# A graph attention kernel: where picked tiles leave their PSUM banks, and where score maxima are issued

## Chip, cores and metric

One core of a Trainium2 chip. The time is that of one execution on the device in microseconds; times are medians of several runs.

## The reference

Three layers of a graph attention over 6250 nodes and 206250 edges, sorted by their target node, with 64 features, then log_softmax, a residual and a layer norm. For each layer, cut to what matters:

```python
q, k, v = x @ Wq + bq, x @ Wk + bk, x @ Wv + bv
e = edge_attr @ We
alpha = sum(q[dst] * (k[src] + e), -1) / sqrt(64)
p = exp(alpha - segment_max(alpha, dst)[dst])
w = p / segment_sum(p, dst)[dst]
x = relu(segment_sum((v[src] + e) * w[:, None], dst) + x @ Ws + bs)   # layer_norm after layers 0 and 1
```

So each edge needs the row of its source node, which is a gather.

## The kernel before

The edges lie in tiles of 128, six tiles to a chunk, four chunks to a **unit**; 67 units of four chunks and a short one go through each layer. The loop over units (line 1883) works on three at a time: for unit u its rows are transposed (`turn`, line 1676 on TensorE, two featT copies on ScalarE, line 1679), for u-1 the scores are made (`scores`, line 1689 on TensorE; a running maximum on VectorE, line 1696, for each half; then the bound, line 1709, and one Exp on ScalarE, line 1710) and turned (`weights`, line 1724; probT, line 1727), and for u-2 the weighted sums are taken (`sums`, line 1736, with the copy of line 1743). Each unit is done in four **quarters**, one chunk's `turn` in each; quarter 2 begins with the first half of `weights`, and ends with the second.

**Where rows come from.** Most tiles are gathered by GpSimd's indirect DMAs (line 601), which wait for a small copy on ScalarE (`gate`, line 633, issued by `free`). But 12 or 14 tiles of a unit (8 in layer 0) are **picked** by TensorE: layer 0 also sorts each chunk's edges so that some tiles hold only sources from a known range of 1024 nodes, whose rows stay in SBUF (`parts`). A VectorE comparison (line 1331, `hot`, issued by `aim`) makes one-hot columns, and a **product** of eight matmuls (line 1388) picks four candidate rows for every edge of two tiles into one PSUM bank. Its **evacuation** (`evacuate`) is a ScalarE copy of candidate 0 (line 1352) and three VectorE predicated copies of the others (line 1355); the bank is free after the last. When a pair of chunks has its last product, three ScalarE copies swap half of the rows (`swap`, lines 1342 to 1344). A unit has 7 or 6 products in layers 1 and 2, two or one to a quarter, and 4 in layer 0, one to a quarter. In layers 1 and 2 products alternate between the two buffers of bank ps_x. In layer 0 ps_x belongs to the sort, and the products of quarters 0 to 3 use ps_p, ps_s, ps_s, ps_p, which are one buffer each and also serve `weights` (ps_p) and `scores` (ps_s).

**What sets the order.** All five engines run in the order in which the program issues; it is written by hand, with generators. `batch` yields after each product; a product's evacuation is issued at the start of the next call, so in front of the next product, wherever that stands, and behind all that was issued between. In layer 0 a generator of the sort (`sorter`, twelve steps a unit, `move(2)` before a quarter's product and `move(1)` after it) is interleaved: a step makes the comparisons `hit` for the step after next, runs six or ten matmuls (lines 1081 and 1090), and every third step copies their banks out on ScalarE (`to`, line 1111, and eT, line 1114), which is the step after a quarter's product. Within it, `mark` computes the edges' positions for four units at once, one piece for each step. Groups of nodes that end (`finish`, by `close_up`) add one step of their own in quarter 0, some on VectorE for about 2 us. `room`, called by `sums`, has SyncE load the edge features for the unit after next into the buffer that `sums` frees.

Of the kernel before, what the change touches and what calls it, by code (L numbers as in the profile page):

```python
# [429 lines left out]
def main_path(  # L430
# [456 lines left out]
    def mark(g):  # L887
# [31 lines left out]
        nc.vector.tensor_tensor(u.rearrange(across, i=HT), adds[:, 0], adds[:, 1], ALU.add)  # L919
        total = ps("a")[0:1, : CELLS * H].rearrange("o (q h) -> o q h", q=CELLS)  # L920
# [375 lines left out]
    class Picker:  # L1296
# [39 lines left out]
        def swap(self):  # L1336

            while self.swaps:
                k, pair, n = self.swaps.pop(0)
                those = loaded[self.layer, k][P // 2 :, 2 * pair : 2 * pair + 2, :n, 0]  # L1340
                spare = stock[0].tile([P, n, D], F32, name="swap", bufs=2)[P // 2 :]
                nc.scalar.copy(spare, those[:, 0])  # L1342
                nc.scalar.copy(those[:, 0], those[:, 1])
                nc.scalar.copy(those[:, 1], spare)

        def evacuate(self):

            if not self.late:
                return
            k, pair, t, px, which, _ = self.late.pop()  # L1350
            found = loaded[self.layer, k][:, 2 * pair : 2 * pair + 2, t, 0]
            nc.scalar.copy(found, px[:, :, 0])  # L1352
            first = t * LB + 2 * pair
            for b in range(1, KB):
                nc.vector.copy_predicated(  # L1355
                    found,
                    which[:, first : first + 2, b].bitcast(I32).unsqueeze(2).to_broadcast([P, 2, D]),
                    px[:, :, b],
                )
            if t == self.plan[k][pair] - 1:  # L1360
                self.swaps.append((k, pair, t + 1))

        def clear(self, bank):

            if self.late and self.late[0][-1] == bank:
                self.evacuate()

# [5 lines left out]
        def batch(self, k):  # L1373

            for pair, most in enumerate(self.plan.get(k, ())):
                for t in range(most):
                    self.swap()
                    self.evacuate()
# [16 lines left out]
                    self.late.append((k, pair, t, px, self.which[k], bank))  # L1395
# [190 lines left out]
    class Unit:  # L1586
# [96 lines left out]
        def scores(self, h, bank):  # L1683
# [3 lines left out]
            for j in range(self.m):  # L1687
                rows = slice(j * W, (j + 1) * W)
                nc.tensor.matmul(p_s[rows, :w], self.q[:, rows], self.featT[j][:, cols], start=True, stop=True)  # L1689
            if h and self.plain and self.k >= NT:  # L1690
                self.turned(0, False)
# [134 lines left out]
    class Line:  # L1826
# [7 lines left out]
        def sums(self, u):  # L1834
# [3 lines left out]
            room(self.layer, u + FB)  # L1838
            self.summed = u + 1

# [4 lines left out]
        def scores(self, u, h, bank="s"):  # L1845
            if u >= 0:
                chunks[self.layer, u].scores(h, bank)

# [25 lines left out]
    for layer in range(L):  # L1874
# [8 lines left out]
        for u in range(NU - 2):  # L1883
# [8 lines left out]
            picker.clear("s")  # L1892
            line.scores(u - 1, 0)
            if waiting:
                active.append(waiting.pop(0))
            for j in range(LB):
                picker.quarter = j
                if j == 2:
                    picker.clear("p")
# [26 lines left out]
            if any(not pair for _, pair, *_ in picker.late + picker.swaps):  # L1926
# [21 lines left out]
        line.sums(u - 2)  # L1948
        line.scores(u - 1, 0)
# [23 lines left out]
        line.sums(u - 1)  # L1973
        line.store()
# [7 lines left out]
        line.sums(u)  # L1982
        line.store()
# [4 lines left out]
        line.sums(u + 1)  # L1988
        line.store()
# [70 lines left out]
```

## Time and profile before

| | us |
|---|---|
| median of 3 runs | 5289.28 |
| the three runs | 5289.01, 5289.28, 5297.1 |
| the profiled execution | 5299.09 |
| its span, first to last instruction | 5297.3 |
| mean granted TensorE clock of it | 0.86 of full speed |

How to read the rows of the profile: a wait row has who waited, its line, for whom and which line, then us in total, how often, and the longest. A row of three or four numbers that begins with a stretch (300.00:2257.00) has the stretch's length, then busy us and instructions of TensorE (PE), its weight loads (PEld), VectorE (DVE), ScalarE (ACT), GpSimd (POOL), then the granted clock, the share of the DMA engines and GB/s. A row of the timeline has start, us, engine, line, what is written from what, shapes, how many of them in a row, and in brackets the idle time before it and who ended it. A group row has busy us, mean ns of one, and idle time before it. DVE and ACT wait rows count idle time, which costs nothing by itself.

### The profile page before, as it was taken

To read this page: it belongs to the slowest core of one execution; us is meant where nothing else is said; L and a number is where in the kernel's file an instruction comes from. 1 tells how busy PE (TensorE), PEld (TensorE's weight loads), DVE (VectorE), ACT (ScalarE), POOL (GpSimd) and SP (SyncE) were. 2 spreads that over 40 slices of the span, in tenths; PEclk is the share of its full clock that TensorE was granted. 3 is DMA by queue.
4 is the path that set the end of the run, shared out by engine and by line. 5 is a ranking of instruction groups with operands and counts; after the bars stand their busy time and mean duration, and the time that the engine had idled before them with its cause. 6 is when DMAs were issued, how large, how long until landed. Compare 5 with 4: busy or idle time off the path is not lost.

```text
span 5297.3 us, 108750 instructions
## 1 busy us (share of the span) xinstructions
PE 3828.8 (72%) x34711; PEld 2753.1 (52%) x34711; DVE 3089.1 (58%) x10790; ACT 2608.1 (49%) x6962; POOL 2677.3 (51%) x2642
## 2 busy tenths in 40 slices
PE   4788777777777777757777776777677676766765
PEld 2344444444444444445566665665456555555554
DVE  6576666667666666634555555555545555555554
ACT  1344444444444444544555555555445555555555
POOL 4464545554544454536555555555275554455552
PEclk9889998899889899977888889888778888888887
DMA  5655555555555555554555555455545555555553
GB/s 121 166 150 149 144 138 144 143 145 139 143 145 144 139 145 144 144 134 123 136 137 144 134 139 143 134 135 139 135 124 140 131 139 134 136 131 137 136 134 85
DMA packets 783506, 728.96 MB, mean 138 GB/s; under 512 B 485192, under 2 KB 610050, under 8 KB 782928
## 3 DMA queue, kind: packets, MB, share of 16 engines
q1 hardware_dynamic: 630436, 508.46, 36.3%
q0 software_dynamic: 84224, 86.41, 8.2%
q10 hardware_dynamic: 68268, 127.03, 6.7%
q8 instruction: 284, 4.65, 0.4%
q14 instruction: 294, 2.41, 0.2%
HBM read 562.78 MB, written 158.68 MB: 136 GB/s over the span
## 4 chain that ended last, share of the span: by engine, by line


## 5 line engine op out<-in xcount | busy, mean ns | idle before, releaser
L601 POOL DMA_INDIRECT feat<-x,gate x1460 | 1460.6, 1000 | 1267.5 <-ACT gate L633 942.3
L1388 PE MATMUL ps_x<-parts,hot 128*128 128x256 f32 x6864 | 1265.8, 339 | 781.7 <-DVE feat L1355 779.2
L601 POOL DMA_INDIRECT feat<-in_x,gate x1100 | 1143.9, 1040 | 1121.2 <-ACT gate L633 701.8
L1388 PEld LDWEIGHTS ps_x<-parts,hot 128*128 128x128 f32 x6864 | 1096.8, 236 | 951.3 <-issue 762.8
L1355 DVE COPY_PREDICATED feat<-which,ps_x 128x128 f32<-128x128 int32 x2574 | 766.8, 300 | 1278.3 <-ACT feat L1352 1137.8
L1679 ACT COPY featT<-ps_a 64x384 f32<-64x384 f32 x1588 | 752.3, 474 | 369.1 <-PE ps_a L1676 357.1
L1676 PE MATMUL ps_a<-ident,feat 128*128 128x128 f32 x2380 | 483.6, 319 | 25.5 <-DMA feat<-x,src_b 23.4
L1070 DVE TENSOR_SCALAR hit<-ruler,pos 128x384 bf16<-128x384 f16 x1608 | 450.4, 323 | 54.2 <-PE ps_m L1090 44.0
L1331 DVE TENSOR_SCALAR hot<-keys,rank 128x512 fp32r<-128x512 f16 (+1 forms) x1172 | 463.1, 463 | 2.5 <-PE ps_x L1388 2.5
L1676 PEld LDWEIGHTS ps_a<-ident,feat 128*128 128x128 f32 x2380 | 327.3, 162 | 203.5 <-issue 180.2
L1727 ACT COPY probT<-ps_p 128x384 f32<-128x384 f32 x399 | 190.6, 478 | 308.1 <-PE ps_p L1724 279.5
L1736 PE MATMUL ps_g<-feat,probT 128*32 128x128 f32 x9672 | 313.1, 276 | 4.5 <-ACT probT L1727 4.5
L1081 PE MATMUL ps_x<-hit,raw 128*64 128x384 bf16 x1608 | 305.6, 375 | 5.2 <-DVE hit L1070 4.9
L1710 ACT ACTIVATE prob<-prob,part 128x768 f32<-128x768 f32 x204 | 190.2, 932 | 203.1 <-DVE part L1709 198.8
L1081 PE MATMUL ps_x<-hit,rest 128*64 128x384 bf16 x1608 | 287.7, 353 | 0.0
L1081 PE MATMUL ps_x<-hit,end 128*64 128x384 bf16 x1608 | 284.9, 350 | 0.0
L1736 PEld LDWEIGHTS ps_g<-feat,probT 128*32 128x32 f32 x9672 | 264.3, 110 | 28.7 <-ACT probT L1727 6.3
L1342 ACT COPY swap<-feat 64x192 f32<-64x192 f32 (+3 forms) x388 | 131.7, 340 | 296.1 <-DVE feat L1355 292.7
L1114 ACT COPY eT<-ps_x 128x384 f32<-128x384 f32 x268 | 129.5, 483 | 299.1 <-PE ps_x L1081 285.7
L1388 PE MATMUL ps_p<-parts,hot 128*128 128x256 f32 x992 | 184.7, 340 | 125.4 <-DVE feat L1355 125.4
L1724 PE MATMUL ps_p<-ident,prob 128*128 128x128 f32 x1197 | 234.2, 312 | 56.0 <-DVE feat L1355 45.6
L1689 PE MATMUL ps_s<-featT,q 128*32 128x384 f32 x2134 | 239.8, 510 | 26.3 <-DVE feat L1355 13.2
(266 smaller groups left out, 5309.4 us busy)
## 6 DMA issues: line engine op xcount, KB each, us to landing
featT<-eaS SPq DMA_DIRECT2D x792, 192.0 KB
feat<-eaP SPq DMA_DIRECT2D x134, 768.0 KB
raw<-in_ea SPq DMA_DIRECT2D x536, 96.0 KB
eaS<-eT ACTq DMA_DIRECT2D x134, 384.0 KB
eaP<-feat ACTq DMA_DIRECT2D x128, 384.0 KB
shade<-maskS SPq DMA_DIRECT2D x198, 192.0 KB
keys<-keyS SPq DMA_DIRECT2D x66, 448.0 KB
keys<-keyS SPq DMA_DIRECT2D x66, 384.0 KB
```

What stands on the lines that cost most here:

```text
L601: nc.gpsimd.indirect_dma_start(out=feat[:, c, t, 0], out_offset=None, in_=xts[layer][:, :], in_offset=bass.IndirectOffsetOnAxis(ap=index[: ...
L1070: nc.vector.tensor_scalar(hit, ruler, self.pos[:, at : at + 1], None, ALU.is_equal)
L1081: nc.tensor.matmul(self.px[j * D : (j + 1) * D, :HE], self.parts[2 * h + i].thirds[part][:, j, t * D : (t + 1) * D], self.hits[h, 2 * i + ...
L1331: nc.vector.tensor_scalar(hot[:, h], keys[self.layer, k][:, first : first + n], rank[:, h : h + 1], None, ALU.is_equal)
L1355: nc.vector.copy_predicated(found, which[:, first : first + 2, b].bitcast(I32).unsqueeze(2).to_broadcast([P, 2, D]), px[:, :, b],)
L1388: nc.tensor.matmul(px[:, v].rearrange("p b d -> p (b d)"), hot[:, h, (2 * pair + v) * P : (2 * pair + v + 1) * P], those[:, i, b0 + h * KB ...
L1676: nc.tensor.transpose(pt[:, t * P : (t + 1) * P], rows[:, 2 * t * D : 2 * (t + 1) * D], ident)
L1679: nc.scalar.copy(featT[:, :, h, :], pt[h * D : (h + 1) * D, : n * P].rearrange("d (i e) -> d i e", e=P))
L1689: nc.tensor.matmul(p_s[rows, :w], self.q[:, rows], self.featT[j][:, cols], start=True, stop=True)
L1724: nc.tensor.transpose(p_t[:, t, :n], self.prob[:n, at : at + P], ident[:n, :n])
L1727: nc.scalar.copy(self.probT[:, t0 : t0 + m, :n], p_t[:, :, :n])
L1736: nc.tensor.matmul(p_g[rows, :].rearrange("n (h d) -> n h d", h=2), self.probT[:, t, rows], batch[:, j, t], start=(t == 0), stop=(t == sel ...
```

## The change

No computation is changed, and the number of instructions of each kind on TensorE, GpSimd and SyncE stays. Six things move:

- In layers 1 and 2 a product's evacuation is issued directly behind the product, and the swap that was due before it behind that (it stays one product late).
- In layer 0 the evacuation is issued at the end of the quarter, after the `move(1)` behind the product, and the products' banks by quarter are ps_p, ps_p, ps_s, ps_p. `clear`, which emptied a bank early where it clashed, goes.
- `scores` is split into `products` (TensorE) and `most` (VectorE's maximum, and after the second half the bound and the Exp). In layers 1 and 2 the first maximum is issued after quarter 0's transposes and gate, the second one with the Exp after quarter 0's products. In layer 0 the first comes after `move(2)` of quarter 0, the second after `move(2)` of quarter 1.
- `mark` yields at four more places, so that VectorE's steps and the matmuls that they feed or wait for are issued one step of the sort apart.
- `room` is called by a new `refill` behind quarter 0's `turn`, no longer in `sums`.

```diff
@@ mark
         nc.vector.tensor_tensor(u.rearrange(across, i=HT), adds[:, 0], adds[:, 1], ALU.add)
+        yield
         total = ps("a")[0:1, : CELLS * H].rearrange("o (q h) -> o q h", q=CELLS)
...
         nc.vector.tensor_reduce(few[:, NW - 1 :, g], sofar[:, NW - 1 :], AX.X, ALU.min)
+        yield
         for i in range(HT):
...
+            yield
             nc.vector.tensor_tensor(ranks[:, i, :CELLS], before, kinds[:, :, i], ALU.mult)
-            yield
...
                 nc.tensor.matmul(taken[:, :, i], ones if j < i else tri, ends_up[:, :, j], start=(j == 0), stop=(j == i))
+        yield
...
+        yield
         nc.vector.tensor_copy(v.rearrange("p (c t) -> p c t", t=TC), place)
@@ Picker
-        def swap(self):
-
-            while self.swaps:
+        def swap(self, left=0):
+
+            while len(self.swaps) > left:
...
                 for t in range(most):
-                    self.swap()
-                    self.evacuate()
+                    if not self.layer:
+                        self.swap()
                     self.aim()
                     at, hot = self.hots[k, t]
-                    bank = "x" if self.layer else "pssp"[self.quarter]
+                    bank = "x" if self.layer else "ppsp"[self.quarter]
...
                         self.free.append(self.hots.pop((k, t))[0])
+                    if self.layer:
+                        due = len(self.swaps)
+                        self.evacuate()
+                        self.swap(len(self.swaps) - due)
                     self.aim()
                     yield
@@ the loop over units
             line.sums(u - 2)
-            picker.clear("s")
-            line.scores(u - 1, 0)
+            line.products(u - 1, 0)
...
                 this.turn(j)
+                if j == 0:
+                    line.refill(u - 2)
                 free(u, j)
                 if j == 0:
                     if layer:
-                        line.scores(u - 1, 1, "m")
+                        line.most(u - 1, 0)
+                        line.products(u - 1, 1, "m")
                     close_up()
...
                 move(pace - pace // 2)
+                if not layer and (not j or j == 1 and placed(0, u + 1)):
+                    line.most(u - 1, j)
                 for _ in range(b - a):
                     next(picking, None)
                 move(pace // 2)
+                if not layer:
+                    picker.evacuate()
                 if j == 0:
-                    if not layer:
-                        line.scores(u - 1, 1)
+                    if layer:
+                        line.most(u - 1, 1)
+                    else:
+                        line.products(u - 1, 1)
+                        if not placed(0, u + 1):
+                            line.most(u - 1, 1)
```

Three places of the order, before and after (the changed kernel's lines are numbered anew: 1356 is the copy that was 1352, 1359 the predicated copies, 1346 to 1348 the swap, 1706, 1719 and 1720 the maxima, the bound and the Exp).

ScalarE at the start of a unit of layer 1, from the copy of the sums on; the first `feat` copy before the change belongs to the last product of the unit before:

```order
L1743 COPY part<-ps_g 128x128
L1679 COPY featT<-ps_a 64x3x128 x2
L633 COPY gate<-src_b 128x6
L1710 ACTIVATE prob,part<-prob,part 128x768
L1352 COPY feat<-ps_x 128x2x64
L1342 COPY swap<-feat 64x192
L1343 COPY feat<-feat 64x192
L1344 COPY feat<-swap 64x192
L1352 COPY feat<-ps_x 128x2x64
L1679 COPY featT<-ps_a 64x3x128 x2
```

And now, where both `feat` copies belong to this unit's own products:

```order
L1753 COPY part<-ps_g 128x128
L1682 COPY featT<-ps_a 64x3x128 x2
L633 COPY gate<-src_b 128x6
L1356 COPY feat<-ps_x 128x2x64
L1346 COPY swap<-feat 64x192
L1347 COPY feat<-feat 64x192
L1348 COPY feat<-swap 64x192
L1356 COPY feat<-ps_x 128x2x64
L1720 ACTIVATE prob,part<-prob,part 128x768
L1682 COPY featT<-ps_a 64x3x128 x2
```

The Exp has moved behind two evacuations and now stands directly ahead of the second quarter's featT copies; the copy of the last unit's last product is gone from here, since it was issued before the sums.

VectorE in a like unit, from the last of the hot tiles that its products use up to those of the next unit (each ISA pair is a score maximum and the reading of its result; the three predicated copies of a product are one after another, so x21 are seven evacuations):

```order
L1331 TENSOR_SCALAR hot_37771<-keys,rank 128x256 x2
L1696 ISA prob,most<-ps_s,shade 128x384
L1696 ISA most 128x1
L1696 ISA prob,most<-ps_m,shade,most 128x384
L1696 ISA most 128x1
L1709 TENSOR_SCALAR part<-most 128x1
L1355 COPY_PREDICATED feat<-which,ps_x 128x2x64 x21
```

And now, with the rows of the same kind:

```order
L1335 TENSOR_SCALAR hot_37775<-keys,rank 128x256 x2
L1706 ISA prob,most<-ps_s,shade 128x384
L1706 ISA most 128x1
L1359 COPY_PREDICATED feat<-which,ps_x 128x2x64 x6
L1706 ISA prob,most<-ps_m,shade,most 128x384
L1706 ISA most 128x1
L1719 TENSOR_SCALAR part<-most 128x1
L1359 COPY_PREDICATED feat<-which,ps_x 128x2x64 x15
```

The second maximum, for which the Exp waits, has moved behind two evacuations, and the last evacuation of a unit now stands ahead of the hot tiles of the next.

ScalarE in layer 0, from the end of quarter 1 to the middle of quarter 2 (`to` and eT are the sort's banks, probT the first half of the weights):

```order
L1111 CAST to<-ps_m 128x12x32
L1114 COPY eT<-ps_x 128x12x32
L1727 COPY probT<-ps_p 128x384
L1679 COPY featT<-ps_a 64x3x128 x2
L633 COPY gate<-src_b 128x6
L1352 COPY feat<-ps_s 128x2x64
```

And now:

```order
L1115 CAST to<-ps_m 128x12x32
L1118 COPY eT<-ps_x 128x12x32
L1356 COPY feat<-ps_p 128x2x64
L1737 COPY probT<-ps_p 128x384
L1682 COPY featT<-ps_a 64x3x128 x2
L633 COPY gate<-src_b 128x6
```

The copy of quarter 1's product has moved ahead of quarter 2's probT, featT and gate, and reads ps_p, the bank that probT's transposes write next.

More of the change, by code (lines that the diff above doesn't have):

```diff
@@ L1349, in evacuate @@
                 return
-            k, pair, t, px, which, _ = self.late.pop()
+            k, pair, t, px, which = self.late.pop()
             found = loaded[self.layer, k][:, 2 * pair : 2 * pair + 2, t, 0]
@@ L1689, in scores, with most @@
                 nc.tensor.matmul(p_s[rows, :w], self.q[:, rows], self.featT[j][:, cols], start=True, stop=True)
+            self.scored = p_s
+        def most(self, h):
+            n, cols = self.rows, self.halves[h]
+            w = cols.stop - cols.start
+            p_s = self.scored
             if h and self.plain and self.k >= NT:
@@ L1837, in sums, with refill @@
             chunks[self.layer, u].sums()
[L1838 removed]
             self.summed = u + 1
+        def refill(self, u):
+            if u >= 0:
+                room(self.layer, u + FB)
         def weights(self, u, h, bank="p"):
@@ L1843, in weights, with products, most, scores @@
                 chunks[self.layer, u].weights(h, bank)
-        def scores(self, u, h, bank="s"):
+        def products(self, u, h, bank="s"):
             if u >= 0:
                 chunks[self.layer, u].scores(h, bank)
+        def most(self, u, h):
+            if u >= 0:
+                chunks[self.layer, u].most(h)
+        def scores(self, u, h, bank="s"):
+            self.products(u, h, bank)
+            self.most(u, h)
         def store(self):
@@ L1925, in main_path @@
             assert next(picking, None) is None
-            if any(not pair for _, pair, *_ in picker.late + picker.swaps):
+            if any(not pair for _, pair, *_ in picker.swaps):
                 picker.flush()
@@ L1948, in main_path @@
         line.sums(u - 2)
+        line.refill(u - 2)
         line.scores(u - 1, 0)
@@ L1973, in main_path @@
         line.sums(u - 1)
+        line.refill(u - 1)
         line.store()
@@ L1982, in main_path @@
         line.sums(u)
+        line.refill(u)
         line.store()
@@ L1988, in main_path @@
         line.sums(u + 1)
+        line.refill(u + 1)
         line.store()
```

6 lines of the change are left out of this document (1 added, 5 removed).

## The prediction

> **What bounds the kernel now.** I read the page first (span, busy shares), then the busy times of three stretches (the loops of layers 0, 1 and 2), then the waits of the whole run.
>
> ```profile
> span 5297.3 us, 108750 instructions
> PE 3828.8 (72%) x34711; PEld 2753.1 (52%) x34711; DVE 3089.1 (58%) x10790; ACT 2608.1 (49%) x6962; POOL 2677.3 (51%) x2642
> 300.00:2257.00 1957.00, 1520.45 (x14411) 913.42 (x14413) 1330.48 (x4715) 948.76 (x2508) 997.55 (x960) 0.90 0.53 145
> 2423.00:3767.00 1344.00, 979.12 (x8821) 812.46 (x8820) 715.00 (x2422) 704.99 (x1947) 715.52 (x713) 0.85 0.52 138
> 3885.00:5242.00 1357.00, 948.33 (x8697) 790.36 (x8696) 717.51 (x2463) 731.93 (x1981) 711.89 (x713) 0.86 0.51 135
> PE ps_x L1388 <- DVE feat L1355: 779.2, 501, 6.3
> PE ps_p L1388 <- DVE feat L1355: 125.4, 59, 4.0
> PE ps_s L1388 <- DVE feat L1355: 121.7, 60, 3.5
> DVE feat L1355 <- ACT feat L1352: 1324.4, 843, 8.2
> L1388 PE MATMUL ps_x<-parts,hot 128*128 128x256 f32 x6864 | 1265.8, 339 | 781.7 <-DVE feat L1355 779.2
> ```
>
> No engine is full. TensorE is busiest, 979 of 1344 us in layer 1, and of the 365 us that it idles there nearly all is one wait: the product of a picked tile (line 1388, eight matmuls, so 6864/8 = 858 products in layers 1 and 2) waits until VectorE has emptied its bank, 779.2 us in the run. VectorE waits in turn for ScalarE's copy (1324 us). So the bound of layers 1 and 2 is the order in which a product is emptied, not a rate. The two loops take 1344 us for 64 units and 1357 us for 65: 21.0 and 20.9 us a unit. A unit has 7 or 6 products. Here is one with 7:
>
> ```profile
> 2793.78 1.19 PE L1388 MATMUL ps_x<-parts,hot 128*128 128x256 f32 x8 [0.58 <-DVE feat L1355]
> 2794.90 1.52 PE L1736 MATMUL ps_g<-feat,probT 128*32 128x128 f32 x48
> 2795.81 2.99 DVE L1331 TENSOR_SCALAR hot<-keys,rank 128x512 fp32r<-128x512 f16 x8
> 2796.24 0.83 PE L1689 MATMUL ps_s<-featT,q 128*32 128x384 f32 x8
> 2797.47 0.85 PE L1689 MATMUL ps_m<-featT,q 128*32 128x384 f32 x8
> 2797.58 0.96 ACT L1679 COPY featT<-ps_a 64x384 f32<-64x384 f32 x2 [0.82 <-PE ps_a L1676]
> 2798.26 1.21 PE L1388 MATMUL ps_x<-parts,hot 128*128 128x256 f32 x8
> 2798.44 0.20 ACT L633 COPY gate<-src_b 128x6 int32<-128x6 int32 x1
> 2798.71 0.55 DVE L1696 CUSTOM_DVE_ANT_0 prob<-ps_s,shade 128x384 f32<-128x384 f32 x1
> 2799.41 0.62 DVE L1696 CUSTOM_DVE_ANT_0 prob<-ps_m,shade,most 128x384 f32<-128x384 f32 x1
> 2800.07 0.15 DVE L1709 TENSOR_SCALAR part<-most 128x1 f32<-128x1 f32 x1
> 2800.26 0.94 ACT L1710 ACTIVATE prob<-prob,part 128x768 f32<-128x768 f32 x1 [1.62 <-DVE part L1709]
> 2801.30 0.27 ACT L1352 COPY feat<-ps_x 128x128 f32<-128x128 f32 x1
> 2801.60 0.97 DVE L1355 COPY_PREDICATED feat<-which,ps_x 128x128 f32<-128x128 int32 x3 [1.37 <-ACT feat L1352]
> 2802.60 0.35 ACT L1342 COPY swap<-feat 64x192 f32<-64x192 f32 x1 [1.03 <-DVE feat L1355]
> 2802.71 2.05 PE L1388 MATMUL ps_x<-parts,hot 128*128 128x256 f32 x8 [3.25 <-DVE feat L1355]
> 2805.15 2.04 PE L1388 MATMUL ps_x<-parts,hot 128*128 128x256 f32 x8
> 2811.03 1.42 PE L1388 MATMUL ps_x<-parts,hot 128*128 128x256 f32 x8
> 2814.93 0.49 PE L1724 MATMUL ps_p<-ident,prob 128*128 128x128 f32 x3
> 2815.26 0.49 PE L1676 MATMUL ps_a<-ident,feat 128*128 128x128 f32 x3
> 2817.63 1.52 PE L1736 MATMUL ps_g<-feat,probT 128*32 128x128 f32 x48
> ```
>
> The last product of the unit before ends at 2794.97, and its copy runs on ScalarE at 2801.30, 6.3 us later: it stands in the queue behind this unit's first featT copies, the gate and the Exp of the scores. The product that needs the bank therefore starts at 2802.71 after 3.25 us of idling.
>
> **Layers 1 and 2.** The change adds and removes no instruction here; it moves the copy and its three predicated copies from the next product's start to right behind their own product, and the second score maximum with its Exp behind the first two of them. I walk the unit above again in the new order, from the rows' durations, 0.1 us a hand-over, all products at 1.2 us. Times are counted from 2794.97.
> - Evacuation of the last product: ScalarE 0.1 to 0.4, VectorE to 1.4. Then `which` and the eight hot tiles (2.99 us) to 4.5, first maximum (0.63 us) to 5.2.
> - First product 3.3 to 4.5 as now. Its copy ends at 4.9, VectorE takes it from 5.2 to 6.2. The second product needs the bank freed at 1.4: 4.5 to 5.7, where it now starts at 7.7. Its copy stands behind the swap (3 x 0.35 us) and ends at 6.4, VectorE at 7.4. Third product, bank free at 6.2: 6.3 to 7.5; now 10.2.
> - Second maximum and bound (0.62 + 0.08 + 0.15 us) to 8.2, Exp to 9.4, **then** featT (0.96), gate (0.20) and the third product's copy, to 10.9; VectorE frees that bank at 11.9. The fourth product runs 7.5 to 8.7, the transposes of prob wait for the Exp (9.3 to 9.8), and the fifth product waits for the bank: 12.0. So it waits about 1.7 us; it starts at 16.1 now. This is what is late next.
> - The last two run on without more than some tenths; the unit ends at 16.6. It takes 22.7 now (2794.90 to 2817.63).
>
> A unit with 6 products has two hot operations less (0.5 us) and no fourth product ahead of the Exp, and walks to 15.4 us, so the mean is 16.0. The same walk in the old order has products start at 3.3, 7.7, 10.4, 12.2, 14.4, 17.2 and 19.8 and ends at 21.0; with 6 it ends at 18.5. That mean is 19.7, where 21.0 is measured: 1.3 us are steps of ending groups and products at 2.05 instead of 1.19 us. I add them back: 17.3, rounded to 17.4. That saves 3.5 us in each of 2 x 66 units: **460 us**, of 779 us that stand in the wait row. Bounds: 0, and 16.0 us a unit (5 x 132 = 660 us) where the additions vanish too.
>
> The next row is the floor under this.
>
> ```profile
> L601 POOL DMA_INDIRECT feat<-x,gate x713 | 715.7, 1004 | 620.8 <-ACT gate L633 462.6 <-issue 143.2 <-ACT feat L1352 9.0
> ```
>
> GpSimd's gathers take (715.7 + 143.2)/64 = 13.4 us a unit with their issue, so they stay hidden while a unit takes over that. SyncE's load of the next edge tiles moves behind one transpose step, about 3 us by the unit above; it is for the unit two later, over 30 us ahead, so I cost it at nothing; without that cover it would be 3 us a unit, 400 us.
>
> The clock: eight matmuls take 1.19 us at the first row of the unit and 2.05 us at 2802.71, right behind the 3.25 us of idling, and the mean is 0.90 in layer 0, which idles less, against 0.85 here. [...]
>
> **Layer 0.** Here one product runs in each quarter of a unit, and the evacuation moves from the next quarter's product to the end of its own quarter, with the banks ps_p, ps_p, ps_s, ps_p for ps_p, ps_s, ps_s, ps_p.
>
> ```profile
> PE ps_p L1388 <- DVE feat L1355: 119.9, 57, 4.0
> PE ps_s L1388 <- DVE feat L1355: 116.6, 58, 3.5
> PE ps_a L922 <- DVE kinds L916: 51.6, 14, 5.1
> PE ps_p L1724 <- DVE feat L1355: 37.8, 45, 2.3
> DVE prob L1696 <- PE ps_s L1689: 228.7, 62, 5.4
> 1500.70 0.48 ACT L1111 CAST to<-ps_m 128x384 bf16<-128x384 f32 x1 [0.41 <-ACT feat L1132]
> 1501.06 0.52 PE L1724 MATMUL ps_p<-ident,prob 128*128 128x128 f32 x3 [0.95 <-DVE feat L1355]
> 1501.08 0.49 ACT L1114 COPY eT<-ps_x 128x384 f32<-128x384 f32 x1
> ```
>
> These waits are from 300 to 2257 us, about 59 units with one of each. The products' own waits (119.9 and 116.6) should go, because a step of the sort now lies between an evacuation and the next product in the same bank; so should the wait of line 922 (51.6), which gets a step of the sort between sums and matmul. One wait grows: the transposes of prob at quarter 2 (line 1724) use ps_p, and its last user is now the product of quarter 1, emptied only just before. Behind the sort's matmuls stand `to` (0.48), eT (0.49), the copy (0.27) and VectorE (0.97), with hand-overs 2.4 us, 59 times 142 us in place of 37.8. Sum: 119.9 + 116.6 + 51.6 - (142 - 37.8) = 184 us. VectorE is busy 68% here and now carries the evacuation at the end of a quarter behind its marking; I take **140 us**, bounds 0 and 230 (half of the new wait). VectorE's 228.7 us on line 1696 I count as nothing: TensorE waits for VectorE in the four rows above and hardly elsewhere. The marking gets four more steps of the sort, of 48 in the four units that it has; steps left over would run at once, which I cost at nothing too.
>
> **Sum.** 460 + 140 = 600 us. The profiled execution took 5299.1 us (span and 1.8 us around it), the median is 5289.3, 0.2% less; the head, the two layer changes and the end are untouched. 5289 - 600 = 4689, say **4690 us**.
>
> **The rivals.**
> - *The waits go almost whole* (0.15): units at 16.0 us and 230 us in layer 0: 890 us, 4400; half-way 4500. For it: nothing else makes TensorE wait in layers 1 and 2. Against it: the Exp chain walked above.
> - *The queue's head moves* (0.18): each copy now blocks ScalarE until its own product ends, and the Exp waits for two evacuations, the hot tiles and a step of an ending group (about 2 us on VectorE). If those 2 us land on the chain in every unit, 19.4 us a unit: 210 us, and with layer 0 at nothing 5080. [...]
> - *Slower* (0.05): the two ps_x banks stop overlapping. If each product had to wait for its predecessor's whole evacuation, it would cost 1.2 + 0.3 + 1.0 + 0.3 = 2.8 us, 6.5 x 2.8 = 18 us, and with 6.2 us of other TensorE work (1.52 + 0.83 + 0.85 + 6 x 0.5) and the 1.3 us 25.7 a unit: 4.7 x 132 = 620 us, 5910. It decides once an evacuation ends later than one product and its transposes. Against it: 2805.15 starts while 2802.71 is not yet emptied.
> - *No change* (0.02): the waits were only the place where another limit showed.
>
> **How the numbers follow.** My forecast, 4590 to 4850, gets 0.60. The range 4450 to 5010 takes in most of the deeper case and a third of the queue's, and leaves out 2 in 10. This kernel's measurement tells about 0.2% from no change; faster by more 0.93, within 0.02, slower 0.05.
>
> **What would show it.** Right: the wait of ps_x for line 1359 (the predicated copies' new line) falls from 779 to some 250 to 350 us and sits at the fifth product; units of about 17.4 us; in layer 0 the transposes of prob wait about 140 us in place of 38. Wrong: units over 19 us with ScalarE waiting for the score bound, or a longer wait for gathers. The forecast fails most easily in the one hand walk, which leaves out ending groups.

## The result and the profile after

The changed kernel takes 4763.52 us (median of four runs, 4757.61 to 4768.13), the kernel before 5293.19 us beside it (5289.01 to 5299.98). The ratio is 0.8998, with a 95% interval of 0.898 to 0.9015: 10% faster, 530 us. The forecast was 4690 us, the range 4450 to 5010.

The page of the changed kernel opens with the span and the busy time of each engine.

```profile
span 4766.3 us, 108288 instructions
PE 3718.2 (78%) x34711; PEld 2645.0 (55%) x34711; DVE 3073.9 (64%) x10790; ACT 2548.1 (53%) x6962; POOL 2659.0 (56%) x2642
```

VectorE, ScalarE and GpSimd do the same work as before (3074 us against 3089 on VectorE). TensorE ran the same 34711 matmuls in 111 us less (3718.2 against 3828.8). To see where, I cut both runs at the first matmul of the sums in each layer, so that a stretch is one layer with the change to the next (the third ends at the sums of the last whole unit but one). First the three stretches of the kernel before, then those of the changed one; the columns are stretch, length, busy time (and instructions) of PE, PEld, DVE, ACT and POOL, granted clock, DMA share and GB/s.

```profile
192.50:2423.10 2230.60, 1701.65 (x15841) 1028.50 (x15833) 1464.03 (x5193) 1057.85 (x2778) 1119.06 (x1080) 0.88 0.53 143
2423.10:3885.50 1462.40, 1048.23 (x9271) 862.50 (x9270) 764.85 (x2594) 751.65 (x2056) 756.88 (x756) 0.83 0.51 136
3885.50:5259.20 1373.70, 958.35 (x8808) 797.43 (x8811) 726.26 (x2491) 740.65 (x2000) 711.70 (x712) 0.86 0.51 134
```

```profile
186.00:2403.50 2217.50, 1765.29 (x15845) 1056.10 (x15838) 1456.87 (x5197) 1051.49 (x2777) 1110.46 (x1078) 0.85 0.53 144
2403.50:3605.80 1202.30, 946.94 (x9271) 779.74 (x9272) 760.90 (x2593) 724.02 (x2057) 747.95 (x754) 0.90 0.63 166
3605.80:4728.40 1122.60, 892.34 (x8808) 747.84 (x8811) 723.12 (x2488) 714.63 (x2002) 709.33 (x716) 0.89 0.63 164
```

Length minus busy time is TensorE's idle time, so each difference splits into idle and busy time; the granted clock stands beside them:

| stage | length | TensorE idle | TensorE busy | clock |
|---|---|---|---|---|
| layer 0 | -13 us | -77 us | **+64 us** | 0.88 to 0.85 |
| layer 1 | -260 us | -159 us | -101 us | 0.83 to 0.90 |
| layer 2 | -251 us | -185 us | -66 us | 0.86 to 0.89 |

Together 524 of the 531 us by which the spans differ. Nearly all of the gain is in layers 1 and 2, and a third of it there (167 of 511 us) is the same matmuls busy for less time. As much lies in the products alone, whose group was busy for 1265.8 us before, at 339 ns a matmul:

```profile
L1387 PE MATMUL ps_x<-parts,hot 128*128 128x256 f32 x6864 | 1096.5, 316 | 307.3 <-DVE feat L1359 184.7 <-ACT feat L1348 116.4 <-ACT feat L1356 3.9
```

In layer 0 TensorE waits 77 us less, and its 15,845 matmuls take 64 us longer.

The waits of the changed kernel, the four longest of TensorE in the whole run (engine, tile and line, who was waited for: total us, times, longest):

```profile
PE ps_p L1734 <- DVE feat L1359: 202.1, 60, 5.1
PE ps_x L1387 <- DVE feat L1359: 184.7, 147, 3.5
PE ps_p L1734 <- ACT prob L1720: 128.0, 107, 3.0
PE ps_x L1387 <- ACT feat L1348: 116.4, 66, 4.1
```

The 779 us of ps_x have become 301 (second and fourth row). The first row is all in layer 0: the transposes of prob, which waited 45.6 us there, now wait 202.1. The third was 7.6 us before: the transposes now wait for the Exp.

One unit of layer 1 with seven products and no step of an ending group, from the timeline (start, duration, engine, line; in brackets the idle time and who ended it):

```profile
2704.35 1.52 PE L1746 MATMUL ps_g<-feat,probT 128*32 128x128 f32 x48
2704.76 0.27 ACT L1356 COPY feat<-ps_x 128x128 f32<-128x128 f32 x1
2706.07 3.17 DVE L1335 TENSOR_SCALAR hot<-keys,rank 128x512 fp32r<-128x512 f16 x8
2707.70 2.17 PE L1387 MATMUL ps_x<-parts,hot 128*128 128x256 f32 x16
2710.75 2.24 PE L1387 MATMUL ps_x<-parts,hot 128*128 128x256 f32 x16 [0.55 <-ACT feat L1356]
2711.56 0.61 DVE L1706 CUSTOM_DVE_ANT_0 prob<-ps_m,shade,most 128x384 f32<-128x384 f32 x1
2712.40 0.94 ACT L1720 ACTIVATE prob<-prob,part 128x768 f32<-128x768 f32 x1 [1.75 <-DVE part L1719]
2713.48 0.55 PE L1734 MATMUL ps_p<-ident,prob 128*128 128x128 f32 x3 [0.49 <-ACT prob L1720]
2714.69 1.84 DVE L1359 COPY_PREDICATED feat<-which,ps_x 128x128 f32<-128x128 int32 x6 [2.33 <-ACT feat L1356]
2715.81 3.59 PE L1387 MATMUL ps_x<-parts,hot 128*128 128x256 f32 x16 [1.45 <-DVE feat L1359]
2719.88 1.19 PE L1387 MATMUL ps_x<-parts,hot 128*128 128x256 f32 x8
2721.00 1.19 PE L1746 MATMUL ps_g<-feat,probT 128*32 128x128 f32 x36
```

The last product's copy runs 0.3 us after the product (2704.76, the product ends at 2704.42) in place of 6.3. The Exp ends at 2713.3, and behind it the fifth product waits 1.45 us. The unit takes 16.65 us (2704.35 to 2721.00). Most units wait longer at the third product; such a unit stands with the account of the prediction.

### The profile page after: what moved, and what is told of

It reads as the page before. It is cut to its first block, busy times and chain, and to the rows that moved or that the text cites. A ratio compares the mean times of both kernels' runs of the same rounds, so it can differ in the third digit from the quotient of the medians.

```text
span 4766.3 us, 108288 instructions
## 1 busy us (share of the span) xinstructions
PE 3718.2 (78%) x34711; PEld 2645.0 (55%) x34711; DVE 3073.9 (64%) x10790; ACT 2548.1 (53%) x6962; POOL 2659.0 (56%) x2642
## 4 chain that ended last, share of the span: by engine, by line
## 5 line engine op out<-in xcount | busy, mean ns | idle before, releaser
L1387 PE MATMUL ps_x<-parts,hot 128*128 128x256 f32 x6864 | 1096.5, 316 | 307.3 <-DVE feat L1359 184.7
L1387 PEld LDWEIGHTS ps_x<-parts,hot 128*128 128x128 f32 x6864 | 987.6, 218 | 410.5 <-issue 156.1
L1734 PE MATMUL ps_p<-ident,prob 128*128 128x128 f32 x1197 | 246.3, 323 | 330.3 <-DVE feat L1359 202.1
L1679 PE MATMUL ps_a<-ident,feat 128*128 128x128 f32 x2380 | 453.7, 303 | 32.2 <-DMA feat<-x,src_b 31.3
L1679 PEld LDWEIGHTS ps_a<-ident,feat 128*128 128x128 f32 x2380 | 308.3, 155 | 210.7 <-issue 181.8
L1734 PEld LDWEIGHTS ps_p<-ident,prob 128*128 128x128 f32 x1197 | 156.6, 162 | 385.9 <-issue 230.1
L1359 DVE COPY_PREDICATED feat<-which,ps_p 128x128 f32<-128x128 int32 x552 | 165.6, 300 | 303.5 <-ACT feat L1356 289.7
L1085 PE MATMUL ps_x<-hit,raw 128*64 128x384 bf16 x1608 | 321.4, 395 | 0.7 <-DVE hit L1074 0.5
L1356 ACT COPY feat<-ps_x 128x128 f32<-128x128 f32 x858 | 221.9, 266 | 175.2 <-PE ps_x L1387 156.5
L1085 PE MATMUL ps_x<-hit,rest 128*64 128x384 bf16 x1608 | 303.9, 374 | 0.0
L1085 PE MATMUL ps_x<-hit,end 128*64 128x384 bf16 x1608 | 301.4, 371 | 0.0
```

The costliest lines, as they stand in the source:

```text
L1085: nc.tensor.matmul(self.px[j * D : (j + 1) * D, :HE], self.parts[2 * h + i].thirds[part][:, j, t * D : (t + 1) * D], self.hits[h, 2 * i + ...
L1359: nc.vector.copy_predicated(found, which[:, first : first + 2, b].bitcast(I32).unsqueeze(2).to_broadcast([P, 2, D]), px[:, :, b],)
L1387: nc.tensor.matmul(px[:, v].rearrange("p b d -> p (b d)"), hot[:, h, (2 * pair + v) * P : (2 * pair + v + 1) * P], those[:, i, b0 + h * KB ...
L1679: nc.tensor.transpose(pt[:, t * P : (t + 1) * P], rows[:, 2 * t * D : 2 * (t + 1) * D], ident)
L1734: nc.tensor.transpose(p_t[:, t, :n], self.prob[:n, at : at + P], ident[:n, :n])
```

## The experiments

Twelve runs. Each is compared with the kernel before on its own chip; "the changed kernel" is 4763.52 us.

**One bank in layer 0.** The transposes of prob at quarter 2 get another bank.

```diff
-                    line.weights(u - 1, 0)
+                    line.weights(u - 1, 0, "p" if layer else "g")
```

> The changed kernel, but in layer 0 the transposes of the first half of prob (quarter 2) write ps_g instead of ps_p, so that they no longer wait for the product of quarter 1 to be emptied. Theory A (layer 0 gave its gain back to this one wait, 196 us between 300 and 2223 us, and to the slower clock behind it): the wait falls under 20 us, the granted clock of layer 0 goes back from 0.87 to 0.90 or more, layer 0 gets 150 to 250 us shorter and the kernel takes 4510 to 4610 us. Rival B (layer 0 is held by VectorE's order, 1330 us busy in 1957 us of before, and TensorE only waits elsewhere): the wait goes, others of the same size come, the kernel stays at 4705 to 4765 us. Rival C (ps_g is not free in time, since ending groups and the sums use it): slower than 4765 us.

Measured: 4531.78 us, ratio 0.8553 (0.853 to 0.8577). Theory A holds. The stretch of layer 0, and the longest wait of TensorE in it:

```profile
188.30:2164.70 1976.40, 1659.33 (x15842) 1000.10 (x15835) 1453.97 (x5195) 1041.19 (x2777) 1138.83 (x1078) 0.91 0.60 161
PE ps_g L1734 <- ACT prob L1720: 47.6, 42, 2.0
```

Against the changed kernel layer 0 is 241 us shorter: 106 us are busy time (1765.29 to 1659.33, the clock 0.85 to 0.91) and 135 idle time. A wait of 202 us cost 241, since with it the same matmuls were busy longer as well. VectorE, at 1454 of 1976 us, is no bound yet, against rival B. A wait of 48 us for the Exp stays where 20 were expected at most.

**The same edit in the kernel before.** If the bank was a bound of its own, it must help there as well.

> The kernel before with only one edit: in layer 0 the transposes of the first half of prob write ps_g instead of ps_p. In the changed kernel this edit alone took 232 us off (4764 to 4532 us). Theory A (the changed order made this wait: in layer 0 it grew from 46 to 202 us and, with the slower clock behind it, took back what the other edits gained): here the edit takes away the 46 us of wait at most and leaves the products' waits of 125 and 122 us, so 5230 to 5290 us on a chip where the kernel before takes 5290 us. Rival (the transposes in ps_p were a bound of their own in both orders, and the change's part in layer 0 is worth nothing): 5050 to 5130 us.

Measured: 5319.62 us, ratio 1.0045 (1.0027 to 1.0063), 25 us slower, and 30 above the upper end of theory A. The rival (5050 to 5130) is out: the wait that costs 241 us is made by the changed order. In the old order waiting only moves. These are the two longest of TensorE in that run's first 2430 us, and its stretch:

```profile
PE ps_s L1388 <- DVE feat L1355: 150.1, 60, 3.5
PE ps_p L1388 <- DVE feat L1355: 125.1, 59, 4.0
192.60:2457.10 2264.50, 1744.17 (x15842) 1056.32 (x15834) 1469.46 (x5195) 1053.33 (x2778) 1130.37 (x1080) 0.86 0.53 141
```

The product in ps_s waits 150 us where it waited 122, and TensorE idles 520 us in place of 529. What makes this kernel slower is busy time: 42 us more, at a clock of 0.86 in place of 0.88. Why, the run does not show.

**One half of the change at a time.** Layer 0 back to the old order (its main lines; the places of the score maxima, of the load by `refill` and of the steps of the positions also go back), then layers 1 and 2 (there too the load goes back).

```diff
-                    bank = "x" if self.layer else "ppsp"[self.quarter]
+                    bank = "x" if self.layer else "pssp"[self.quarter]
...
                     if not self.layer:
                         self.swap()
+                        self.evacuate()
...
-                if not layer:
-                    picker.evacuate()
```

> Layer 0 as before (order, banks, position steps), layers 1 and 2 as changed. Theory A (the two halves of the change are independent and layer 0's half is worth 10 us): 4760 to 4785 us. Rival (layer 0's edits gain more than the loop's 10 us show, for instance in how the loops join): over 4800 us. Rival (layer 0's edits cost something): under 4755 us.

```diff
-                    if not self.layer:
-                        self.swap()
+                    self.swap()
+                    if self.layer:
+                        self.evacuate()
...
-                    if self.layer:
-                        due = len(self.swaps)
-                        self.evacuate()
-                        self.swap(len(self.swaps) - due)
...
             line.products(u - 1, 0)
+            if layer:
+                line.most(u - 1, 0)
...
-                        line.most(u - 1, 0)
                         line.products(u - 1, 1, "m")
+                        line.most(u - 1, 1)
...
-                    if layer:
-                        line.most(u - 1, 1)
-                    else:
+                    if not layer:
```

> Layers 1 and 2 as before, layer 0 as changed. Theory A: 5265 to 5290 us, the loop of layer 0 at 2104 us, the loops of layers 1 and 2 at 1344 and 1357 us. Rival (a part of the 502 us comes from what layer 0 leaves behind, or from the clock of the whole run): under 5200 us.

Measured: 4796.35 us, 0.9055 (0.9036 to 0.9073), without layer 0's half, and 5257.38 us, 0.9931 (0.9909 to 0.9953), without the other. Both miss their windows by 8 to 11 us on the side that gives layer 0 more: its half is worth 33 us by the first (4796.35 less 4763.52) and 36 by the second (5293.83 less 5257.38), not the 13 that one pair of profiles shows. The halves add up (36 and 497, against 530), so they are independent. The stretch of layer 0 without the other half is 2206.00 us long with TensorE busy for 1740.43, at a clock of 0.87: 25 us less than in the kernel before, again with less idling and more busy time.

**Which edit of layers 1 and 2.** Copies at once, but both score maxima and the Exp right behind their products, as before:

```diff
             line.products(u - 1, 0)
+            if layer:
+                line.most(u - 1, 0)
...
-                        line.most(u - 1, 0)
                         line.products(u - 1, 1, "m")
+                        line.most(u - 1, 1)
...
-                    if layer:
-                        line.most(u - 1, 1)
-                    else:
+                    if not layer:
```

> The changed kernel, but in layers 1 and 2 both score maxima and the Exp are issued right behind their products again, as before; the picked tiles are still copied at once. Theory A (the first copies of a unit stood behind the Exp; with the Exp ahead of them again, the copy of the first product waits for Exp, about 2 to 3 us a unit, but the last product of the unit before is emptied at once): units of 18.5 to 19.5 us, 4950 to 5080 us. Rival D (only the early copy matters): within 30 us of the changed kernel's 4764 us. Rival E (the order of the score maxima is the whole of it): over 5200 us.

Measured: 4768.32 us, 0.8992 (0.8956 to 0.9027): rival D, the changed kernel's time. Theory A's range begins 182 us higher. Four of its waits of TensorE, the three longest among them:

```profile
PE ps_x L1387 <- ACT feat L1348: 312.5, 104, 6.4
PE ps_p L1734 <- DVE feat L1359: 201.1, 60, 5.1
PE ps_x L1387 <- DVE feat L1359: 56.5, 17, 4.3
PE ps_p L1734 <- ACT prob L1720: 15.9, 9, 3.1
```

The transposes hardly wait for the Exp (15.9 us for 128.0), and the products wait 369 us for 301: the copies stand behind the Exp instead. In one unit the first product ends at 3056.49 and the Exp starts at 3057.43; the product's copy runs behind the Exp and an activation of an ending group (1.28 us of it the load of its table), at 3060.10, and the third product starts at 3061.51, after 3.74 us of idling. What the order of the maxima gives at one place it takes at the other.

The other way round, the maxima in the new order and the copies late (the first two pieces of the diff of layers 1 and 2 above):

> The changed kernel, but in layers 1 and 2 the picked tiles are copied late again, at the start of the next product, as before; the second score maximum and the Exp stay behind the first two products of the unit. Theory A (the 6.3 us that a copy stood in ScalarE's queue were the Exp of the scores ahead of it; either edit puts the copy ahead of the Exp): 4780 to 4950 us, the wait of ps_x for the predicated copies well under 500 us. Rival F (the gain needs the copy right behind its product): 5200 to 5290 us with some 750 us in that wait.

Measured: 5922.47 us, beside 5962.9 us of the kernel before, ratio 0.9931 (0.9907 to 0.9954). The kernel before takes some 12% longer on that chip than on the others (the last section). Once more:

> The kernel scores_only once more: the call that had it ran on a chip on which the kernel before took 5963 us, where TensorE paused within its 48-matmul blocks. Changed kernel, but in layers 1 and 2 the picked tiles are copied at the start of the next product, as before. Theory A (the Exp of the scores ahead of the copy in ScalarE's queue is the cause; either edit cures it): 4780 to 4950 us. Rival F (the gain needs the copy right behind its product): 5200 to 5290 us, with some 750 us in the wait of ps_x for the predicated copies. The other chip's trace has 696 us in that wait, which speaks for F.

The same chip: 5883.3 us beside 5914.02, ratio 0.9938 (0.9915 to 0.9962). These ratios decide nothing, since on that chip kernels that copy at once, with the better bank in layer 0 besides, reach only 0.98 and 1.00 (the next two runs), where the bank alone gave 0.855 on another. The idle time before the products does decide. Their group, first here, then in the next run on that chip, which copies at once:

```profile
L1388 PE MATMUL ps_x<-parts,hot 128*128 128x256 f32 x6864 | 1280.7, 342 | 836.3 <-DVE feat L1359 709.8 <-issue 115.1 <-remote 6.7
```

```profile
L1387 PE MATMUL ps_x<-parts,hot 128*128 128x256 f32 x6864 | 1138.4, 323 | 335.5 <-DVE feat L1359 202.1 <-ACT feat L1348 90.6 <-issue 34.1
```

With late copies it is 836 us, with copies at once 336. So rival F holds for the wait: the new order of the maxima does not shorten it, and theory A, that only the Exp held up the copies, is wrong. What this order is worth in time was not measured on a chip like the others. In one unit of its trace three copies are late in three ways. That of the product which ends at 3213.23 runs at 3219.14, behind the next unit's first featT copies, with no Exp between. That of the next product (it ends at 3219.56) runs at 3221.80, behind a swap that waits 1.25 us for VectorE. That of the third (it ends at 3221.97) runs at 3225.81, behind the Exp and two featT copies. In all three, what the program issues ahead of the next product ran first on ScalarE.

**Towards a faster kernel.** With the bank in layer 0, two edits in layers 1 and 2 were tried on what still waits: the step of an ending group behind the Exp, and the hot tiles made one by one.

```diff
                         line.products(u - 1, 1, "m")
-                    close_up()
+                    else:
+                        close_up()
...
                     if layer:
                         line.most(u - 1, 1)
+                        close_up()
```

> The changed kernel with the transposes of prob in ps_g in layer 0, and in layers 1 and 2 the step of an ending group moved behind the second score maximum and the Exp. Base: 4532 us with ps_g alone. Theory A (the ending step's VectorE and ScalarE instructions stand ahead of the second copy and of the Exp, about 2 us in each of the units that have one, some 60 of 132): 4400 to 4490 us. Rival (the step delays something in any place): 4515 to 4550 us.

```diff
+            done = 0
-            while self.free and self.todo and (self.layer, self.todo[0][0]) in self.ready:
+            while self.free and self.todo and (self.layer, self.todo[0][0]) in self.ready and not (self.layer and done):
+                done += 1
```

> The changed kernel with the transposes of prob in ps_g in layer 0, and in layers 1 and 2 the hot tiles made one at a time (two operations, 0.75 us) in place of all four ahead of the first score maximum (3 us). Base: 4532 us with ps_g alone. Theory A (the Exp, for which the transposes of prob wait 110 us in layers 1 and 2, and the first copies come 1 to 2 us earlier): 4380 to 4490 us. Rival (VectorE's copies now stand behind the hot tiles instead, the wait only moves): 4510 to 4560 us.

These two and the next ran on the slow chip again: ratios 0.9838 (0.9785 to 0.9892) and 0.9984 (0.996 to 1.0009). Neither can be held against 4532 us, so what each is worth alone stays open. Both together (the ending step now behind the unit's first products), with the maxima right behind their products as in the evac_only run:

> As the two before together (ps_g, hot tiles one at a time, the ending step behind the first two products), and with both score maxima and the Exp right behind their products again, so that the Exp runs first and only the copies of the first products stand behind it. Theory A (with the hot tiles out of the way the Exp ends 5 us into the unit, no transposes wait for it, and a copy waits for it at most 1 us): 4330 to 4450 us. Rival (ScalarE's queue: the first copies wait behind the Exp, as in the kernel before, 2 us a unit): 4500 to 4700 us.

On the slow chip 5771.18 us, ratio 0.9678 (0.9631 to 0.9725). Again:

> The kernel evac_fin_w0g once more, for the same reason: ps_g for the transposes of prob in layer 0; in layers 1 and 2 hot tiles one at a time, both score maxima and the Exp right behind their products, the ending step behind the first two products, copies at once. Theory A (the Exp ends early, no transposes wait for it, a copy waits for it at most 1 us): 4330 to 4450 us, against 4532 us with ps_g alone. Rival (ScalarE's queue: the first copies wait behind the Exp, 2 us a unit): 4500 to 4700 us.

The same chip: 5721.1 us, 0.9672 (0.9631 to 0.9714). A third time:

> The kernel evac_fin_w0g a third time, since the two calls that had it ran on a chip on which the kernel before took over 5900 us. On a chip where the kernel before takes about 5290 us: theory A (hot tiles one at a time and the ending step behind the first products let the Exp end early, no transposes of prob wait for it and a copy waits for it at most 1 us): 4330 to 4450 us, against 4532 us with ps_g alone. Rival (the first copies wait behind the Exp in ScalarE's queue, 2 us a unit): 4500 to 4700 us. On the slower chip: 5700 to 5780 us again.

On another chip, with the kernel before at 5299.42: 4521.37 us, ratio 0.853 (0.8504 to 0.8556). The interval overlaps that of the bank alone (0.853 to 0.8577), so nothing is gained that can be measured; theory A's 4330 to 4450 fell, and the time lies in the rival's range. These are the waits of TensorE that matter here, over the whole run:

```profile
PE ps_x L1389 <- DVE feat L1361: 188.5, 141, 3.9
PE ps_s L1694 <- issue: 62.1, 25, 5.4
PE ps_x L1389 <- ACT feat L1358: 60.9, 90, 1.4
PE ps_x L1389 <- DVE hot L1337: 58.3, 128, 1.8
PE ps_s L1694 <- DMA featT<-eaS: 24.1, 14, 3.4
PE ps_p L1736 <- ACT prob L1722: 9.0, 5, 2.6
```

The transposes wait 9 us for the Exp in place of 125, but the products wait 308 us (188.5, 60.9 and 58.3) where they waited 303 with the bank alone, now in part for hot tiles, and the score products (ps_s) wait 86 us (62.1 and 24.1) for loads or for nothing shown, where they waited 19 with the bank alone. The fastest kernels are these two, 4532 and 4521 us; the first differs from the changed kernel in one bank.

## Why the prediction was right, and where it was wrong

*Products of layers 1 and 2: right in size, wrong in place.* The step said that the wait of 779 us falls to 250 to 350 and sits at the fifth product. It is 301 us, and the unit shown above fits the walk: its fifth product waits 1.45 us (forecast 1.7), and it takes 16.65 us (walk 16.6). But that unit is not the usual one. Counted over the 128 units of the two loops in the timeline, TensorE idles 224 us before the third product, which the walk had starting 0.6 us after the second, and 79 us before the fifth. In 95 units the third product waits over 1 us, 207 us together, and in each of these VectorE or ScalarE is at instructions of an ending group in between. Here is one, the unit from 2687.32 to 2704.35:

```profile
2690.67 2.16 PE L1387 MATMUL ps_x<-parts,hot 128*128 128x256 f32 x16
2691.92 0.27 ACT L1356 COPY feat<-ps_x 128x128 f32<-128x128 f32 x1 [0.86 <-PE ps_x L1387]
2692.50 1.09 DVE L1474 TENSOR_SCALAR y<-y,mv,dev 128x64 f32<-128x64 f32 x4
2693.62 0.89 DVE L1479 TENSOR_TENSOR y<-y,gb 128x256 f32<-128x256 f32 x2
2694.48 1.83 DVE L1359 COPY_PREDICATED feat<-which,ps_x 128x128 f32<-128x128 int32 x6
2695.60 2.05 PE L1387 MATMUL ps_x<-parts,hot 128*128 128x256 f32 x8 [2.43 <-DVE feat L1359]
```

The first product's copy is done at 2692.19, and VectorE comes to it at 2694.48, behind the layer norm of an ending group (lines 1474 and 1479). The walk left these steps out, so it was partly luck that the total fell into the forecast range. In the fastest kernel, where the step stands behind the first two products, the same count gives 67 us before the third product and 170 before the fifth: the wait moved.

That evacuating at once is the cause, two runs show: alone, with the maxima as before, it gives the whole gain (4768 against 4764 us), and without it the wait is back in either order of the maxima (with the new one 836 us of idling before the products, beside 336 on the same chip; with the old one, layers 1 and 2 undone, a wait of 787 us).

*The unit's length: right by two misses that cancel, which is luck.* Forecast 17.4 us, 460 us saved; measured 17.1 and 17.3 us over the two loops, 511 us saved over the stretches. (Both loops have 64 units, so the second took 21.2 us a unit before, not 20.9.) The walk had all of it in waiting, 3.7 us a unit, with the 1.3 us for slow matmuls and ending steps left nearly whole. Measured: 344 us less idling, 2.6 us a unit, and 167 us less busy time, 1.3 us a unit. Idling fell by less than walked, since the walk left out ending groups and gave the wait for the Exp (128 us) too little weight. The products' matmuls gave what the sum had denied them: they are busy for 169 us less (1265.8 to 1096.5). The products wait less (301 us for 779), and the clock rose from 0.83 and 0.86 to 0.90 and 0.89. The prediction's two clocks, 0.90 in layer 0, which idled less, against 0.85 in layer 1, pointed this way, but its sum took nothing from them.

*Layer 0: the step that failed.* The prediction put it so: "One wait grows: the transposes of prob at quarter 2 (line 1724) use ps_p, and its last user is now the product of quarter 1, emptied only just before", priced at 2.4 us, "59 times 142 us in place of 37.8", sum 184, taken as 140 us. The mechanism was right and its size was not: 13 us by the profiles, 33 to 36 by the halves. Term by term in the stretch of layer 0: the two products' waits of 125 and 122 us went, as forecast. The wait of the transposes rose to 202 us, 3.4 each. Line 923's wait fell from 54.8 to 32.6 us, where all of it was to go. That makes 113 us; new small waits leave 77 of them. And the busy time rose by 64 us, a term that the sum did not have. Why 3.4 and not 2.4 us, these rows of the changed kernel show; TensorE falls idle at 1129.14.

```profile
1128.65 0.93 ACT L1720 ACTIVATE prob<-prob,part 128x768 f32<-128x768 f32 x1 [0.93 <-DVE part L1719]
1129.59 0.46 ACT L1136 COPY feat<-ps_a 128x384 f32<-128x384 f32 x1
1130.08 0.37 ACTq L1144 DMA_DIRECT2D eaP<-feat  x1
1130.49 0.48 ACT L1115 CAST to<-ps_m 128x384 bf16<-128x384 f32 x1 [0.44 <-ACT feat L1136]
1130.86 0.48 ACT L1118 COPY eT<-ps_x 128x384 f32<-128x384 f32 x1
1131.23 0.28 ACT L1356 COPY feat<-ps_p 128x128 f32<-128x128 f32 x1
1131.55 0.97 DVE L1359 COPY_PREDICATED feat<-which,ps_p 128x128 f32<-128x128 int32 x3 [2.47 <-ACT feat L1356]
1132.66 0.88 PE L1734 MATMUL ps_p<-ident,prob 128*128 128x128 f32 x3 [3.52 <-DVE feat L1359]
```

The sum counted from `to` (1130.49) on, and from there it is 2.2 us. Ahead of it in ScalarE's queue stand the Exp, which the change itself had put into this quarter with the second maximum, a copy of line 1136 and the issue of its store. Counted over the 60 waits in the timeline, the Exp runs within the idle time in 37, which are 3.9 us long on average; the other 23 are 2.5. With the transposes in another bank, layer 0 gains 254 us (2230.6 to 1976.4).

*The rest.* What lies outside the three stretches moved by 7 us of 531. SyncE's load behind the transposes cost next to nothing (the score products waited 6.0 us for featT in the whole run). The rival of the queue's head shows in the evac_only run: the Exp and the copies take each other's time in ScalarE's queue, though at no loss in sum (4768 us against 4764). The products still overlap (in the unit shown above two run in 2.17 us from 2707.70, and the first one's copy starts only at 2708.96), so the slower case did not come.

## What to carry to other kernels

When a wait is taken away, price what is late next from the whole queue of the engine that ends it, with all that the same change moves into that queue, and not from the last few instructions. Split a measured difference into idle time and busy time of TensorE by stage: here both the missing gain of layer 0 and a third of the gain elsewhere were busy time, which a walk through waits cannot see. A buffer that two users share in turn is worth trying in another place before anything is rescheduled: one bank was worth 232 us here, though in the order before the same bank made the kernel 25 us slower.

## What the runs showed of the hardware

*The clock did not follow the idle time.* Layer 0 in four orders; the pauses are the gaps between TensorE's rows in the timeline.

| layer 0 in | idle us | pauses over 2 us | busy us | clock |
|---|---|---|---|---|
| kernel before | 529 | 82 | 1702 | 0.88 |
| before, ps_g | 520 | 116 | 1744 | 0.86 |
| changed | 452 | 91 | 1765 | 0.85 |
| changed, ps_g | 317 | 32 | 1659 | 0.91 |

From the kernel before to the changed one TensorE idles less (529 to 452 us) and runs slower (0.88 to 0.85). The row with the fewest pauses over 2 us, 32, has the highest clock, 0.91, and the 82 of the kernel before stand beside 0.88; but 116 stand beside 0.86 and 91 beside 0.85, so the two do not go in step. What lowers the clock there is not settled.

Nor did the busy time follow the mean clock in layer 1. Here it is with the bank alone, and in the fastest kernel (on another chip):

```profile
2164.70:3377.30 1212.60, 954.11 (x9268) 783.48 (x9267) 759.55 (x2593) 724.39 (x2057) 749.31 (x754) 0.89 0.64 164
2164.90:3344.50 1179.60, 949.81 (x9271) 747.34 (x9274) 767.24 (x2593) 732.64 (x2058) 740.16 (x755) 0.94 0.68 169
```

The clock is 0.05 higher, and the same matmuls are busy for 4 us less of 954.

*One chip was slower, and TensorE paused inside its blocks there.* The group of the sums' matmuls, first in the changed kernel, then on that chip (fin_w0g):

```profile
L1746 PE MATMUL ps_g<-feat,probT 128*32 128x128 f32 x9672 | 312.8, 276 | 0.8 <-ACT probT L1737 0.8
```

```profile
L1746 PE MATMUL ps_g<-feat,probT 128*32 128x128 f32 x9672 | 725.6, 316 | 520.4 <-issue 505.7 <-ACT featT L1682 2.5 <-ACT probT L1737 2.3
```

The same 9672 matmuls had 520 us of idling ahead of them where there had been 0.8, "issue" meaning that nothing which the profile shows was waited for. The kernel before took 5914 to 5963 us on it. What was slow there was not found. It does not hit all kernels alike: the kernel before takes some 12% longer there, the fastest kernel 27% (5721 against 4521 us), and with the copies late the same matmuls of the sums had 147 us of idling ahead of them, in the scores_only run's repeat. So ratios from that chip are not those of the others.
